# An eight-expert attention model on one core: scores in halves of 64 keys, expert columns prepared earlier, the last division in pieces

## The chip, the cores and the metric

The kernel runs on one core of a Trainium2 chip. The metric is device time in microseconds of one execution. A core has five engines with a queue each: TensorE (PE in the profile, with its weight loads apart as PEld), VectorE (DVE), ScalarE (ACT), GpSimd (POOL) and SyncE (SP). Products go from PE into PSUM, eight banks of 512 float32 per partition; everything else lies in SBUF or in the chip's main memory.

## What is computed

The input is one image of 256 channels and 64 by 64 pixels. Layer 0 is a linear attention over boxes of pixels, layer 1 a softmax attention over all 4096 tokens and a mixture of eight experts with two experts per token.

```python
# layer 0
x = x + L0_conv(_gn(x))               # q, k sigmoid, v normalized; for boxes of 64, 32, 16 pixels:
                                      #   attn = q . box(k v) / (q . box(k) + 1e-6); then Wout
# layer 1
t = _to_tokens(x)                     # 4096 tokens of 256
t = t + L1_attn(_ln_t(t))
t = t + L1_ffn(_ln_t(t))
...
# L1_attn, 8 heads of 32
qkv = x @ w_qkv + b_qkv
dots = einsum('bhid,bhjd->bhij', q, k) * d ** -0.5
out = softmax(dots) @ v ;  return out @ w_out + b_out
# L1_ffn, 8 experts, 2 per token
logits = xt @ Wr + br
xe = xn * ln_g[e] + ln_b[e]
h = gelu(xe @ W1[e] + b1[e]);  y = h @ W2[e] + b2[e]
out = sum over the two best experts of weight * y
```

Everything is float32.

## The kernel before

**Order of the work.** The code states the work in program order; a planner then orders each engine's queue by its own estimates, so that neighbouring steps of independent work may stand in the queue in another order than in the code. `tc.issue_after` ties an instruction behind another one of its engine. Waits between engines are semaphores. What stands inside a branch isn't mixed with what stands outside.

**Layer 0** (`prepare`, `attend`) runs twice, for four heads each time (g = 0, 1). `prepare` makes q, k, v and sums by boxes. `attend` walks over three box sizes and computes scores of key tiles against strips of query columns, four heads at a time: head h has its 32 channels on partitions 32h to 32h + 31, so that the four heads' products use four row groups of PE. Strips are packed into steps of at most 512 columns. One part (L612, box sizes with r above 1) computes scores 64 keys at a time, since keys of the upper and the lower half of a tile have different queries. The other part (L681) computes 128 keys at a time. `masked` (L557, L561) multiplies the scores by masks on DVE, ACT and POOL, and `use` (L643, L697) multiplies by v. In the L681 part a step consists of one or two pieces: those of 384 or 512 columns stand alone, those of 192 and 256 share a step.

**Layer 1, q, k, v.** For eight chunks c of 512 tokens: normalize, transpose (`to_channels`, L779 and L780), project q and k (L885, copied out by L889), project v together with the router's columns (L896, L903, L904). This part has a pool of PSUM tiles `mm` of four banks and a pool `a_in` called `win`. At its end a bound on all scores is computed and read into a register, `tame`.

**Layer 1, attention.** A branch on `tame` holds two versions; the first one runs with this input. It has 16 blocks, one for each chunk of 512 queries (qc) and each group of four heads (g). A block walks over 32 key tiles i. Per tile:

```python
sc = [two_banks() for _ in range(2)]          # 2 of 3 double banks
for hd in range(4):
    nc.tensor.matmul(sc[hd // 2][:, hd % 2, :], qk[hs, 1, g, tok(i)], qk[hs, 0, g, chunk(qc)], ...)   # L994
for pair, s in zip(pairs, sc):
    nc.scalar.activation(pe[:, pair, :], s, AF.Exp, ...)                                              # L1004
for pair in pairs:
    add = nc.vector.tensor_add(total[:, pair, :], ..., pe[:, pair, :])                                # L1011, i = 1 to 30
```

The values' product `use` (L962, into `ps_acc`) of a tile is emitted one tile later, by `tick`. `pe` has four buffers, `total` one. For the softmax's denominators, the last tile's `pe` (in `take`) and then `total` (in `whole`) are multiplied by ones into `ps_den` (both L962). `take` also copies the accumulator to `attnT` (L1029). For 15 blocks the denominators then travel through main memory to be inverted compactly (`pack`, `turn`, `spread`, L1050 to L1063). For the last block `divide` inverts them at once: one reciprocal of 128 by 512 (L1040) and one product (L1035), and then `project` runs for the last four token tiles (L943, L946, and the statistics of the second normalization, L764 and L765). Of the other 28 token tiles four are projected in each block with g = 1 from qc = 1 on.

**Behind the branch.** The phase of the experts begins with constants (L129), the router's bias `br` (L151) and a block named `routing`. That one first loads three matrices of the experts (b1, ln_g, ln_b) as rows, transposes them on PE (L1207), copies them on DVE (L1208) into `cols`, and stores `cols` to main memory as `crows` (L1212), from where each slot of the expert phase loads its expert's columns (L1184). Then come the second normalization (`norm2.begin`: L769 and the square root L770; `end`: L773), the normalized rows (L1229) and their store `zrows`, the choice of two experts per token, the places of all tokens in the slots (L1352 to L1401), and the expert phase proper (L1413 to L1466) with the final sum and transposes.

**What ACT's tables need.** Exp, square root, sigmoid and gelu each make ACT load a table when the function before was another one (ACT_TABLE_LOAD in the profile).

Of the kernel before, what the change touches and what calls it, by code (L numbers as in the profile page):

```python
# [22 lines left out]
F32 = mybir.dt.float32  # L23
# [7 lines left out]
P = 128  # L31
# [83 lines left out]
def tile_conv_attn_hybrid(ctx: ExitStack, tc: tile.TileContext, a: dict, out: bass.AP):  # L115
# [73 lines left out]
    with ExitStack() as phase:  # L189
# [394 lines left out]
        def attend(g, work, ps, qk, v, ssum, rec, woT):  # L584
# [6 lines left out]
            for w in (2, 1, 0):  # L591
# [71 lines left out]
                for ix in range(NCH):  # L663
# [12 lines left out]
                    for step in steps:  # L676
                        scs = [score() for _ in range(4)]
                        at, places = 0, []
                        for n, i, c0, c1, *mk in step:
                            for h in range(4):  # L680
                                nc.tensor.matmul(  # L681
                                    scs[h][:, at : at + n],
                                    kT[hs[h], tok(i)],
                                    qT[hs[h], CH * ix + CELL * c0 : CH * ix + CELL * c1],
                                    start=True,
                                    stop=True,
                                    skip_group_check=True,
                                )
                            places.append((at, n, i, c0, c1, *mk))
                            at += n  # L690
                        sms = masked(work, scs, at, joined((p[0], p[1], *p[-2:]) for p in places))
                        step_done()

                        def use(places=places, sms=sms, acc=acc, begun=begun, ix=ix, last=step is steps[-1], raw=raw, r=r):
                            for at, n, i, c0, c1, *_ in places:
                                for h in range(4):
                                    nc.tensor.matmul(  # L697
                                        acc[hs[h], CELL * c0 : CELL * c1],
                                        v[:, i, hs[h]],
                                        sms[h][:, at : at + n],  # L700
                                        start=not begun[0],
                                        stop=last and at == places[-1][0],
                                        skip_group_check=True,
                                    )
                                begun[0] = True
                            if last and r > 1:
                                nc.vector.tensor_add(raw[:, ix, :], acc, raw[:, ix, :])
                            elif last:
                                nc.scalar.copy(raw[:, ix, :], acc)

                        behind(lambda: None, use)
# [68 lines left out]
        nc.scalar.copy(dst, tp[:, :C].rearrange("p (k n) -> p k n", k=KC))  # L780

    norm2 = Norm(keep, "ln2")


    with ExitStack() as phase:
# [15 lines left out]
        with (  # L801
# [61 lines left out]
            for c in range(NCH):  # L863
# [29 lines left out]
                for i in range(NB * c, NB * (c + 1)):  # L893
# [8 lines left out]
                        )  # L902
                    nc.vector.tensor_add(v[:, i, :], pv[:, :C], bv)  # L903
                    nc.scalar.copy(t[:, i, C:], pv[:, C : C + NE])  # L904


            on_experts = lambda z: z.unsqueeze(2).to_broadcast([P, NT, NE])
# [41 lines left out]
        with tc.If(tame > 0) as branch:  # L949
            with (  # L950
# [33 lines left out]
                for qc in range(NCH):  # L984
                    for g in range(KC):
# [4 lines left out]
                        for i in range(NT):  # L990
                            sc = [two_banks() for _ in range(2)]
                            for hd in range(4):
                                hs = slice(D * hd, D * (hd + 1))
                                nc.tensor.matmul(  # L994
                                    sc[hd // 2][:, hd % 2, :],
                                    qk[hs, 1, g, tok(i)],
                                    qk[hs, 0, g, chunk(qc)],
                                    start=True,
                                    stop=True,
                                )  # L1000
                            pe = work.tile([P, 4, CH], F32, name="pe", bufs=4)
                            pairs = [slice(0, 2), slice(2, 4)]
                            for pair, s in zip(pairs, sc):
# [20 lines left out]
                            if i == NT - 1:  # L1024
# [9 lines left out]
                                def times(rec, to=to):  # L1034
                                    nc.vector.tensor_mul(to, to, rec)  # L1035

                                def divide(den=den, whole=whole, times=times):
                                    whole()
                                    rec = work.tile([P, CH], F32, tag="rec", name="rec")
                                    nc.vector.reciprocal(rec, den[0])  # L1040
                                    times(rec)

# [100 lines left out]
    with ExitStack() as phase:  # L1145
# [3 lines left out]
        small = pool("m_small", 1)  # L1149


        cst.update(constants_of("m", wts))
        zrows = dram.tile([N, C], F32, name="zrows")
        yrows = dram.tile([2 * N + NU * P, C], F32, name="yrows")


        crows = dram.tile([NE, P, NH + 2 * KC], F32, name="crows")
        br = row_on_all("L1_ffn_br", NE, wts)

        def each(name):  # L1160
# [34 lines left out]
        with ExitStack() as routing:  # L1195
# [1 line left out]
            r_ps = routing.enter_context(psum("r_ps", 2))  # L1197
            bank, _ = banks(r_ps)
            r_work = pool("r_work", 2)

            cols = r_work.tile([P, NE, NH + 2 * KC], F32, name="cols", bufs=1)
            at = 0
            for name, n in (("L1_ffn_b1", NH), ("L1_ffn_ln_g", KC), ("L1_ffn_ln_b", KC)):
                rw = r_work.tile([NE * n, P], F32, tag="rw", name=f"{name}_rows")
                nc.scalar.dma_start(rw, a[name].rearrange("e (k p) -> (e k) p", p=P))
                tp = bank()
                nc.tensor.transpose(tp[:, : NE * n], rw, ident[: NE * n, : NE * n])  # L1207
                nc.vector.tensor_copy(  # L1208
                    cols[:, :, at : at + n], tp[:, : NE * n].rearrange("p (e k) -> p e k", e=NE)
                )  # L1210
                at += n
            nc.scalar.dma_start(crows.rearrange("e p n -> p e n"), cols)  # L1212

# [331 lines left out]
```

## Time and profile before

| | |
|---|---|
| median of 3 runs | 2913.63 us (2911.81 to 2914.61) |
| profiled execution: its time | 2911.62 us |
| its span, first to last instruction | 2909.8 us |
| layer 0 | 0 to 1029 us |
| q, k, v of layer 1 | 1029 to 1153 us |
| attention, with the last projections | 1153 to 2325 us |
| routing | 2325 to 2371 us |
| experts and output | 2371 to 2910 us |
| PE busy, share of the span | 2769.2 us, 95% |
| DVE busy | 2082.3 us, 72% |
| ACT busy | 1529.6 us, 53% |
| POOL busy | 712.4 us, 24% |

How to read the profile: times are microseconds of one profiled execution. A group's row gives the line, the engine, the operation, output and inputs by the program's names, the shapes and the number of instructions; behind the first bar stand the busy time in all and the mean nanoseconds of one; behind the second the time that the engine sat idle just before these instructions, and what ended it. A timeline's row gives start, length, engine, line and operation, the number of merged instructions, and in brackets the idle time ahead of it. A float32 matmul of the code appears as two MATMUL records[...], each with a weight load of its own (LDWEIGHTS on PEld). Matmuls overlap, so that their lengths don't add up. Instants of single instructions are given from the start of the span.

### The profile page before, as it was taken

To read this page: it belongs to the slowest core of one execution; us is meant where nothing else is said; L and a number is where in the kernel's file an instruction comes from. 1 tells how busy PE (TensorE), PEld (TensorE's weight loads), DVE (VectorE), ACT (ScalarE), POOL (GpSimd) and SP (SyncE) were. 2 spreads that over 40 slices of the span, in tenths; PEclk is the share of its full clock that TensorE was granted. 3 is DMA by queue.
4 is the path that set the end of the run, shared out by engine and by line. 5 is a ranking of instruction groups with operands and counts; after the bars stand their busy time and mean duration, and the time that the engine had idled before them with its cause. 6 is when DMAs were issued, how large, how long until landed. Compare 5 with 4: busy or idle time off the path is not lost. (4 is left out here: it accounts for less than half of the span.)

```text
span 2909.8 us, 62928 instructions
## 1 busy us (share of the span) xinstructions
PE 2769.2 (95%) x26286; PEld 1329.9 (46%) x26286; DVE 2082.3 (72%) x3009; ACT 1529.6 (53%) x2134; POOL 712.4 (24%) x808
## 2 busy tenths in 40 slices
PE   6899999989999988999999999999999969999996
PEld 5466442735644254222222222222222248888884
DVE  6776777577676886999999999999999941111113
ACT  3242323124233312888888888888888642222222
POOL 1085858109485711000000000000000012222220
PEclk9999999999999999999999999999999969999997
DMA  5000000000000000000000000000000056565665
GB/s 143 6 2 3 2 3 2 7 0 3 4 2 3 1 19 1 1 5 6 5 5 5 5 5 5 5 5 5 5 5 5 10 176 215 190 203 196 205 213 189
DMA packets 97546, 136.31 MB, mean 47 GB/s; under 512 B 18115, under 2 KB 79145, under 8 KB 97253
## 3 DMA queue, kind: packets, MB, share of 16 engines
q1 hardware_dynamic: 82360, 105.34, 11.2%
q0 software_dynamic: 6528, 17.83, 2.2%
q10 hardware_dynamic: 8364, 9.02, 0.9%
q8 instruction: 209, 3.42, 0.5%
q14 instruction: 85, 0.69, 0.1%
HBM read 114.57 MB, written 17.60 MB: 45 GB/s over the span
## 5 line engine op out<-in xcount | busy, mean ns | idle before, releaser
L1004 ACT ACTIVATE pe<-ps_two 128x1024 f32<-128x1024 f32 x1024 | 993.1, 1022 | 152.2 <-PE ps_two L994 146.9
L1011 DVE TENSOR_TENSOR total<-total,pe 128x1024 f32<-128x1024 f32 x928 | 1058.2, 1219 | 2.2 <-ACT pe L1004 2.2
L994 PE MATMUL ps_two<-qk 32*128 32x512 f32 x4096 | 630.6, 640 | 3.5 <-POOLq L949 1.8
L962 PE MATMUL ps_acc<-pe,v 128*32 128x512 f32 x4096 | 547.2, 605 | 0.1
L557 ACT COPY sm<-ps_sc 128x384 f32<-128x384 f32 (+4 forms) x486 | 232.5, 513 | 460.6 <-PE ps_sc L681 271.2
L561 POOL TENSOR_TENSOR sm<-sm,mask 128x192 f32<-128x192 f32 (+3 forms) x460 | 380.2, 860 | 232.7 <-ACT sm L557 232.5
L994 PEld LDWEIGHTS ps_two<-qk 32*128 32x128 f32 x4096 | 205.2, 183 | 419.5 <-PE ps_two L994 221.3
L561 DVE TENSOR_TENSOR sm<-ps_sc,mask 128x384 f32<-128x384 f32 (+3 forms) x708 | 324.1, 518 | 92.8 <-PE ps_sc L681 91.4
L1456 ACT ACTIVATE hid<-ps_hp,cols 128x256 f32<-128x256 f32 (+1 forms) x288 | 133.1, 462 | 360.4 <-PE ps_hp L1453 359.3
L1271 POOL MEMSET on<- 128x256 f32 x1 | 0.3, 311 | 1177.3 <-PE ps_den L962 1177.3
L962 PEld LDWEIGHTS ps_acc<-pe,v 128*32 128x32 f32 x4096 | 80.8, 108 | 390.3 <-issue 377.2
L681 PE MATMUL ps_sc<-qk 32*128 32x192 f32 (+3 forms) x2688 | 245.3, 446 | 5.7 <-DVE sm L561 2.9
L1453 PE MATMUL ps_hp<-xe,w 128*128 128x256 f32 (+1 forms) x1152 | 246.6, 370 | 0.0
L1462 PE MATMUL ps_yp<-w,hid 128*128 128x256 f32 x1088 | 240.8, 379 | 0.0
L1453 PEld LDWEIGHTS ps_hp<-xe,w 128*128 128x128 f32 x1152 | 201.1, 190 | 39.7 <-ACT hid L1456 5.6
L697 PE MATMUL ps_acc<-sm,v 128*32 128x192 f32 (+3 forms) x2688 | 216.6, 423 | 0.8 <-POOL sm L561 0.8
L1462 PEld LDWEIGHTS ps_yp<-w,hid 128*128 128x128 f32 x1088 | 204.2, 190 | 26.4
L1432 DVE TENSOR_SCALAR xe<-ps_tp,cols 128x256 f32<-128x256 f32 (+1 forms) x72 | 34.8, 525 | 239.3 <-PE ps_tp L1428 217.5
L561 POOL TENSOR_TENSOR sm<-sm,ycut 128x384 f32<-128x384 f32 (+4 forms) x150 | 150.8, 1024 | 140.9 <-ACT sm L557 140.6
L681 PEld LDWEIGHTS ps_sc<-qk 32*128 32x128 f32 x2688 | 126.3, 186 | 124.5 <-DVE sm L561 70.1
L561 DVE TENSOR_TENSOR sm<-ps_sc,ycut 128x512 f32<-128x512 f32 (+4 forms) x250 | 127.7, 562 | 65.2 <-PE ps_sc L612 63.2
L1464 DVE TENSOR_TENSOR y<-ps_yp,b 128x256 f32<-128x256 f32 x68 | 28.9, 425 | 195.1 <-PE ps_yp L1462 195.1
(239 smaller groups left out, 2244.3 us busy)
## 6 DMA issues: line engine op xcount, KB each, us to landing
w<-in_L_ffn_W SPq DMA_DIRECT2D x72, 1024.0 KB
b<-in_L_ffn_b SPq DMA_DIRECT2D x36, 128.0 KB
rows<-in_x SPq DMA_DIRECT2D x16, 256.0 KB
zrows<-act SPq DMA_DIRECT2D x4, 1024.0 KB
y<-yrows SPq DMA_DIRECT2D x8, 512.0 KB
y<-yrows ACTq DMA_DIRECT2D x8, 512.0 KB
rec<-recs SPq DMA_DIRECT2D x60, 64.0 KB
x<-in_x ACTq DMA_DIRECT2D x4, 512.0 KB
```

What stands on the lines that cost most here:

```text
L557: nc.scalar.copy(sm[:, :used], sc[:, :used])
L561: engine.tensor_mul(to, of, mk.unsqueeze(1).to_broadcast(list(to.shape)))
L681: nc.tensor.matmul(scs[h][:, at : at + n], kT[hs[h], tok(i)], qT[hs[h], CH * ix + CELL * c0 : CH * ix + CELL * c1], start=True, stop=True, ...
L697: nc.tensor.matmul(acc[hs[h], CELL * c0 : CELL * c1], v[:, i, hs[h]], sms[h][:, at : at + n], start=not begun[0], stop=last and at == plac ...
L962: nc.tensor.matmul(to[D * hd : D * (hd + 1), :], lhsT(hd), rhs[:, hd, :], start=start, stop=stop, skip_group_check=True,)
L994: nc.tensor.matmul(sc[hd // 2][:, hd % 2, :], qk[hs, 1, g, tok(i)], qk[hs, 0, g, chunk(qc)], start=True, stop=True,)
L1004: nc.scalar.activation(pe[:, pair, :], s, AF.Exp, scale=C**-0.5)
L1011: add = nc.vector.tensor_add(to, first[:, pair, :] if i == 1 else to, pe[:, pair, :])
L1432: nc.vector.tensor_scalar(xe[:, k, :n], tp[:, k, :n], cols[:, gain], cols[:, shift], op0=ALU.mult, op1=ALU.add,)
L1453: nc.tensor.matmul(hp[:, :n], w1[:, k, tok(m)], x_now[:, k, :n], start=k == 0, stop=k == KC - 1)
L1456: nc.scalar.activation(hid[:, m, :n], hp[:, :n], AF.Gelu, bias=cols[:, m : m + 1])
L1462: nc.tensor.matmul(yp, hid[:, m, tok(j)], w2[:, m, :], start=m == 0, stop=m == NH - 1)
```

## The change

Five edits:

1. In layer 0 a step of the L681 part with a single piece computes its scores in two halves of 64 keys; steps with two pieces stay at 128.
2. In the attention each head's scores (L994) are computed in two halves of 64 keys. The tiles in PSUM stay as they were.
3. The last block's division runs in four pieces of 128 queries, each a reciprocal and a product.
4. The experts' columns leave the routing. A function `expert_columns` loads, transposes, copies (now on ACT) and stores them after chunk c = 2 of the q, k, v part, with loads and the store in SP's queue and PSUM tiles from the four banks `mm`.
5. The first instruction behind the branch on ACT is a square root of one element, `root`.

```diff
                         for n, i, c0, c1, *mk in step:
+
+                            rows = CELL if len(step) == 1 else P
                             for h in range(4):
-                                nc.tensor.matmul(
-                                    scs[h][:, at : at + n],
-                                    kT[hs[h], tok(i)],
...
+                                for u in range(0, P, rows):
+                                    nc.tensor.matmul(
+                                        scs[h][u : u + rows, at : at + n],
+                                        kT[hs[h], P * i + u : P * i + u + rows],
...
+    def expert_columns(pool, ps):
+        cols = pool.tile([P, NE, NH + 2 * KC], F32, name="cols")
+        at = 0
+        for name, n in (("L1_ffn_b1", NH), ("L1_ffn_ln_g", KC), ("L1_ffn_ln_b", KC)):
+            rw = pool.tile([NE * n, P], F32, name=f"{name}_rows")
+            nc.sync.dma_start(rw, a[name].rearrange("e (k p) -> (e k) p", p=P))
+            tp = ps.tile([P, CH], F32, tag="mm", name="ps_mm")
+            nc.tensor.transpose(tp[:, : NE * n], rw, ident[: NE * n, : NE * n])
+            nc.scalar.copy(cols[:, :, at : at + n], tp[:, : NE * n].rearrange("p (e k) -> p e k", e=NE))
+            at += n
+        nc.sync.dma_start(crows.rearrange("e p n -> p e n"), cols)
...
+                if c == 2:
+                    expert_columns(win, ps)
...
-                                nc.tensor.matmul(
-                                    sc[hd // 2][:, hd % 2, :],
-                                    qk[hs, 1, g, tok(i)],
...
+                                for u in range(2):
+                                    nc.tensor.matmul(
+                                        sc[hd // 2][CELL * u : CELL * (u + 1), hd % 2, :],
+                                        qk[hs, 1, g, P * i + CELL * u : P * i + CELL * (u + 1)],
...
                                     rec = work.tile([P, CH], F32, tag="rec", name="rec")
-                                    nc.vector.reciprocal(rec, den[0])
-                                    times(rec)
+                                    for n in range(CH // P):
+                                        nc.vector.reciprocal(rec[:, tok(n)], den[0][:, tok(n)])
+                                        nc.vector.tensor_mul(to[:, tok(n)], to[:, tok(n)], rec[:, tok(n)])
...
+        root = small.tile([1, 1], F32, name="root")
+        nc.scalar.sqrt(root, ident[:1, :1])
...
-            for name, n in (("L1_ffn_b1", NH), ("L1_ffn_ln_g", KC), ("L1_ffn_ln_b", KC)):
-                rw = r_work.tile([NE * n, P], F32, tag="rw", name=f"{name}_rows")
-                nc.scalar.dma_start(rw, a[name].rearrange("e (k p) -> (e k) p", p=P))
-                tp = bank()
-                nc.tensor.transpose(tp[:, : NE * n], rw, ident[: NE * n, : NE * n])
-                nc.vector.tensor_copy(
...
-            nc.scalar.dma_start(crows.rearrange("e p n -> p e n"), cols)
```

## The prediction

> **What bounds the kernel now.** I read the page first, then the table of stretches, the groups of the attention stretch, the timelines of VectorE and TensorE at one block's end, two score steps of layer 0, and the stretch behind the attention. The head of the page:
>
> ```profile
> span 2909.8 us, 62928 instructions
> ...
> PE 2769.2 (95%) x26286; PEld 1329.9 (46%) x26286; DVE 2082.3 (72%) x3009; ACT 1529.6 (53%) x2134; POOL 712.4 (24%) x808
> ```
>
> TensorE (PE) looks like the bound of everything. In the table of stretches, however, from 1600 to 1900 us PE is busy for all 300.00 us and VectorE (DVE) for 291.90. A PE busy without a gap can be waiting inside, so the attention (1153 to 2319 us, 40% of the span) needs a closer look. Its groups:
>
> ```profile
> L1011 DVE TENSOR_TENSOR total<-total,pe 128x1024 f32<-128x1024 f32 x928 | 1058.2, 1219 | 2.2 <-ACT pe L1004 2.2
> L1004 ACT ACTIVATE pe<-ps_two 128x1024 f32<-128x1024 f32 x1024 | 993.1, 1022 | 152.2 <-PE ps_two L994 146.9
> L994 PE MATMUL ps_two<-qk 32*128 32x512 f32 x4096 | 630.6, 640 | 3.5 <-POOLq L949 1.8 <-ACT pe L1004 1.6
> L962 PE MATMUL ps_acc<-pe,v 128*32 128x512 f32 x4096 | 547.2, 605 | 0.1
> ```
>
> The 928 running sums of L1011 waited 2.2 us in all: inside a block (one qc, one g, 32 key tiles) DVE never waits. It waits only at a block's end, where `total` must be read by PE before the next block overwrites it:
>
> ```profile
> 1247.40 47.77 DVE L1011 TENSOR_TENSOR total<-total,pe 128x1024 f32<-128x1024 f32 x42
> 1296.98 2.36 DVE L1011 TENSOR_TENSOR total<-pe 128x1024 f32<-128x1024 f32 x2 [1.81 <-ACT pe L1004]
> ```
> ```profile
> 1292.81 1.04 PE L962 MATMUL ps_den<-pe,ones 128*32 128x512 f32 x8
> 1293.78 1.14 PE L994 MATMUL ps_two<-qk 32*128 32x512 f32 x8
> 1294.85 1.06 PE L962 MATMUL ps_acc<-pe,v 128*32 128x512 f32 x8
> 1295.73 1.04 PE L962 MATMUL ps_den<-total,ones 128*32 128x512 f32 x8
> 1296.70 1.14 PE L994 MATMUL ps_two<-qk 32*128 32x512 f32 x8
> ```
>
> The last sum ends at 1295.17. PE, which works through its queue without a gap, reaches the products that read `total` at 1295.73, 0.56 us late, and DVE starts again 1.25 us after that. So the attention is DVE's sums end to end, plus a gap at each of 15 block ends, part of which is PE being late. The waits list has these gaps as 29.8 us (13 times) behind `pe` and 7.4 (4 times) behind `ps_den`; without the 6.1 us before the first sum and the 2.2 above, 29 us for 15 ends: 2.73 at the first, 1.78 to 2.06 at the others.
>
> Layer 0 (0 to 1029 us) is PE's. Its scores exist in both forms, 64 keys at a time (L612) and 128 (L681), here both with 384 query columns:
>
> ```profile
> 385.25 0.90 PE L612 MATMUL ps_sc<-qk 32*64 32x384 f32 x16
> 386.08 0.98 PE L643 MATMUL ps_acc<-sm,v 64*32 64x448 f32 x16
> ```
> ```profile
> 475.99 0.93 PE L681 MATMUL ps_sc<-qk 32*128 32x384 f32 x8
> 476.84 1.07 PE L697 MATMUL ps_acc<-sm,v 128*32 128x512 f32 x8
> ```
>
> From a step's start to the next line's is 0.83 us with 64 keys, 0.85 with 128, though there are twice the instructions. Behind the attention DVE carries the chain:
>
> ```profile
> 2315.24 3.36 DVE L1040 RECIPROCAL rec<-ps_den 128x512 f32<-128x512 f32 x1 [1.15 <-PE ps_den L962]
> 2318.71 0.69 DVE L1035 TENSOR_TENSOR act<-act,rec 128x512 f32<-128x512 f32 x1
> ...
> 2324.68 0.30 DVE L765 BATCH_NORM_AGGREGATE ln_mv<-st 128x2 f32<-128x6 f32 x2
> ...
> 2327.72 0.17 DVE L1283 TENSOR_SCALAR steps<-cstm 128x16 f32<-128x16 f32 x1 [2.74 <-issue]
> ...
> 2328.13 0.31 DVE L1208 COPY cols<-ps_mm 128x64 f32<-128x64 f32 x2 [0.24 <-DMA L_ffn_ln_b_rows<-in_L_ffn_ln_b]
> 2328.35 0.17 DVE L769 TENSOR_SCALAR ln_rstd<-ln_mv 128x32 f32<-128x32 f32 x1
> ```
>
> **What the Trainium skill says.** "TensorE: Matmul & The Clock Gate", LDWEIGHTS (loading the stationary operand): a load takes columns/1.2 ns, whatever the rows. That is 107 ns for 128 columns, 53 for 64, 27 for 32. The trace agrees: an f32 product runs as two passes, and in L994 the second starts 533 ns after the first (427 of stream, 106 of load), in L962 454 after (427 and 27), in L612 with 448 columns 427 after (373 and 54). The same page, The mechanism: a load overlaps running matmuls only in other row groups. The trace agrees for the first pass to the second, but from the second pass on a step's further loads are hidden (162 ns from pass to pass at 192 columns, with either form). "TensorEngine Tiling (Array Packing)", Instruction Overhead: about 60 cycles per matmul. The trace is far below that: matmuls on different tiles start 6.7 ns apart, in L612 eight in 47 ns. "ScalarE: Activation LUTs", What ACT_TABLE_LOAD costs: 1283 ns and a drain; the load before the root at 2326.05 us took 1.28.
>
> **Scores in the attention, removed and added.** Each of 512 iterations exchanges 8 matmuls with 128-column loads for 16 with 64-column loads. Between the passes 107 − 53 = 54 ns go. As eight matmuls start over 47 ns instead of four over 20, the last one ends 27 ns later, and the next kind starts 91 ns behind the end of the last stream in both forms. PE saves 54 − 27 = 27 ns per iteration; single starts at 384 columns give 857 − 831 = 26. Heads 2 and 3 often start later than 0 and 1 because they wait for exp; a pair then has its second matmul's stagger only, so up to 40 ns are saved. Over 32 iterations that is 0.8 to 1.3 us per block. DVE's sums don't get shorter (960 × 1.14 us), so it can be cashed only at the block ends: with PE there in time, the gap is 1.25 us plus some 0.05 for the signal, 1.30. The fourteen later gaps, 26.3 us together, lose 26.3 − 14 × 1.30 = 8.1, needing 0.5 to 0.8 us of PE per block, which it has. The first end (2.73, PE slowed at the start) is limited by PE and gets about 1.0. **−9.1 us**; bounds −10 and, should PE's saving be eaten elsewhere, 0.
>
> **Scores in layer 0.** Only steps of one piece are split: 80 of 384 columns and 32 of 512 (640 and 256 matmul records by 8). 112 × 26 ns = 2.9. In 48 of them heads 2 and 3 wait some 0.07 to 0.2 us for their bank, so a part comes back as waiting. **−2.5**, bounds −3.5 and 0.
>
> **Last division in pieces.** A reciprocal costs 0.553 us at 64 columns (L345) and 3.353 at 512 (L530), by interpolation 0.95 at 128; a product of 128 columns 0.29 (L1287), the hand-over 0.11 (2318.71 − 2318.60), less some 0.05 of overlap: 1.3 per piece, 5.2 for four against 4.16. DVE is through at 2320.4 instead of 2319.4. But PE may start the first of the last four token tiles at 2316.6. Before, these tiles took DVE from 2319.40 to 2324.98, of which 1.06 + 0.45 + 0.75 us went in waiting for PE; 3.3 us are work. 2320.4 + 3.3 = 2323.7: **−1.2**, bounds 0 (if the pieces' small hand-overs cost double) and −2.3.
>
> **Columns moved out of the routing.** Three copies, three transposes, three row loads and the store of `crows` leave. L769, the first step of the chain to the routing, stood behind the copies at 2328.35; it can start at about 2327.85, behind the 2.74 us that DVE stands still after the branch and which stay. One later copy (0.17 us, 0.12 from start to start) also lay in the chain. **−0.6**, bounds 0 and −1.
>
> **Columns added at c = 2.** PE is busy 18.97 of 20 us from 1060 on; three transposes at 0.17 us from start to start (L1207) are **+0.5**, bounds 0 and +1.5 (each also holds one of four banks till ACT has copied it). The three copies (0.2 us each) lie on an ACT that is busy 2.8 of 20 us. The four DMAs go to SP's queue, which is empty between the weights at 1029.86 and the attention's own from 1225 on; nobody behind them waits. Without that cover the rows' 2 to 3 us to land would stand before the first transpose.
>
> **Root behind the branch.** The table load before, at 2326.05, ended 1.2 us ahead of L769's result, so it was hidden; earlier it is hidden too: 0. ACT has only the load of `br` queued behind it, needed at 2329.95. If the 1.28 us ever lay open, that is its price.
>
> **Sum.** −9.1 − 2.5 − 1.2 − 0.6 + 0.5 = −12.9 us. The profiled execution has a span of 2909.8 and took 2911.62: 2896.9 and 2898.7. Its time lies 2.0 under the median of the runs shown, 2913.63; against that median the forecast is **2900.7**.
>
> **The rivals.** First, the attention gives nothing: PE's 27 ns disappear in its loop with exp, and the gaps stay at 1.8. Speaking for it: ACT waited 146.9 us for scores, PE's score loads waited behind other scores 221.3 us, so the loop has its own rhythm (2.16 us per iteration against 2.07 of PE's work). Against: that rhythm contains the shortened pass. It gives 2913.6 − 3.8 = 2909.8. Second, only half comes: 2905. Third, on the other side: the planner that orders each engine's queue sees eight score products for four, counts PE as slower than it is, and puts the products of `total` one iteration later. (That it reorders shows at 1030 us, where two L764 stand before two L765 though the code alternates.) Each of 15 ends would then cost one more turn of scores and values, 2.1 us: +31 − 3.8, thus 2941; even a fifth of the ends misplaced would eat most of the rest. Against it: at every end the products stand directly behind the values, as written. Fourth, the split doesn't do what it says, because eight streams of 512 columns don't run side by side; then 0.43 us more per pass, hundreds of us. L612 with 448 columns excludes it nearly: less than 1 in 100.
>
> **Numbers.** Forecast 0.72; half 0.10; nothing in the attention 0.10; planner 0.05; every bound on the good side (−16.8, about 2897), 0.03. A measurement of this kernel can't tell 0.2% (5.8 us) from no change, so the line lies at 2907.8. Faster are the forecast, the half and the best case, 0.85; same 0.10; slower 0.05. The range reaches from 2895.0 (all bounds good, less the 1.8 us by which the lowest run lies under the median) to 2908.5, beyond the half and short of the first rival.
>
> **What would show it.** Second pass of L994's successor 480 ns after the first; gaps before `total<-pe` of 1.3 instead of 1.8 to 2.0; DVE's sums unchanged in number and at 1.14 us; a single-piece step of 384 columns 0.83 us long; 8.5 us from the last division's first reciprocal to the last L765 instead of 9.7; L769 directly behind `steps`. Wrong would make it: gaps still at 1.8, a DVE that waits inside a block, or L994's two passes still 533 apart.

## The result and the profile after

| kernel | median us | range, runs | ratio to the kernel before |
|---|---|---|---|
| before | 2912.81 | 2910.74 to 2914.61, 6 | |
| changed | 2902.53 | 2899.56 to 2903.15, 6 | 0.9962 [0.9950, 0.9975] |

The change saves 10.3 us; 12.9 were forecast. The heads of the pages, after:

```profile
span 2900.4 us, 73149 instructions
...
PE 2758.0 (95%) x31278; PEld 1283.2 (44%) x31278; DVE 2081.5 (72%) x3012; ACT 1529.1 (53%) x2138; POOL 712.6 (25%) x808
```

There are 10,221 instructions more. The groups of the attention stretch (busy, mean ns of one, then idle time ahead and who ended it):

```profile
L1035 DVE TENSOR_TENSOR total<-total,pe 128x1024 f32<-128x1024 f32 x928 | 1058.1, 1215 | 1.2 <-ACT pe L1028 1.1
L1028 ACT ACTIVATE pe<-ps_two 128x1024 f32<-128x1024 f32 x1023 | 991.5, 1021 | 144.0 <-PE ps_two L1017 128.2 <-DVE total L1035 0.2
L1017 PE MATMUL ps_two<-qk 32*64 32x512 f32 x8168 | 619.1, 613 | 1.8 <-ACT pe L1028 1.8
L983 PE MATMUL ps_acc<-pe,v 128*32 128x512 f32 x4096 | 547.1, 605 | 0.1
```

The sums (L1035, before L1011) and the values (L983, before L962) are as they were; the scores have twice the records. In the trace's single starts the second pass of the scores begins 480 ns behind the first where nothing holds it (533 before). The end of the second block (the one shown of before), on DVE and on PE (start, length, then idle time ahead):

```profile
1250.23 47.78 DVE L1035 TENSOR_TENSOR total<-total,pe 128x1024 f32<-128x1024 f32 x42
1299.22 2.36 DVE L1035 TENSOR_TENSOR total<-pe 128x1024 f32<-128x1024 f32 x2 [1.21 <-PE ps_den L983]
```
```profile
1295.77 1.11 PE L1017 MATMUL ps_two<-qk 32*64 32x512 f32 x16
1296.81 1.07 PE L983 MATMUL ps_acc<-pe,v 128*32 128x512 f32 x8
1297.69 1.42 PE L983 MATMUL ps_den<-total,ones 128*32 128x512 f32 x8
1299.04 1.11 PE L1017 MATMUL ps_two<-qk 32*64 32x512 f32 x16
```

The last sum ends at 1298.01. PE reaches the products of `total` at 1297.69, ahead of it, and has to wait for it: the eight last 1.42 us instead of 1.04. The gap is 1.21 us instead of 1.81. At the later ends PE is still just too late: the products start 0.10 us (g = 0) and 0.20 us (g = 1) behind the last sum, typically 0.56 and 0.74 before. The gaps are 1.26 and 1.43 us there, 2.69 at the first end, and the 15 add up to 21.4 us, 29.0 before. One single-piece step in layer 0, followed by its neighbour's values:

```profile
449.97 0.90 PE L684 MATMUL ps_sc<-qk 32*64 32x384 f32 x16
450.80 0.77 PE L643 MATMUL ps_acc<-sm,v 64*32 64x320 f32 x16
```

From start to start 0.83 us, as forecast. Behind the attention:

```profile
2310.50 1.77 DVE L1065 RECIPROCAL rec<-ps_den 128x128 f32<-128x128 f32 x2 [1.18 <-PE ps_den L983]
2312.18 0.42 DVE L1066 TENSOR_TENSOR act<-act,rec 128x128 f32<-128x128 f32 x2
...
2317.35 0.30 DVE L768 BATCH_NORM_AGGREGATE ln_mv<-st 128x2 f32<-128x6 f32 x2
2320.32 0.17 DVE L1296 TENSOR_SCALAR steps<-cstm 128x16 f32<-128x16 f32 x1 [2.67 <-issue]
2320.40 0.17 DVE L772 TENSOR_SCALAR ln_rstd<-ln_mv 128x32 f32<-128x32 f32 x1
```

From the first reciprocal to the last L768 (before L765) 7.15 us pass, 9.74 before; L772 (before L769) stands directly behind `steps`, as the forecast wanted it.

**Stage by stage.** The runs of this study leave different parts of the code as before, so each stage can be read from several profiles. A stage runs from one marker to the next: layer 0 from its first score to the last sum of its output product; q, k, v to the attention's first score; the attention to the last division's first reciprocal; the division to the last L765 or L768; the last one to the first row that ACT normalizes with `less`.

```
stage            forecast  profiles with the old code  profiles with the new code    difference
layer 0            -2.5    888.5 (5: 884.6 to 892.1)   888.4 (7: 886.0 to 889.9)       -0.1
q, k, v            +0.5    117.5 (5: 116.7 to 118.5)   118.7 (8: 117.9 to 119.6)       +1.2
attention          -9.1    1167.5 (2: 1167.0, 1168.0)  1159.9 (9: 1157.8 to 1161.4)    -7.6
division           -1.2    8.94 (5: 8.18 to 9.74)      7.15 (9: all 7.15)              -1.8
to the routing     -0.6    7.05 (5: 6.99 to 7.20)      6.61 (9: 6.44 to 7.21)          -0.4
```

The sum is -8.7; the two profiles' spans differ by 9.4 and the medians by 10.3. One code's profiles spread by 1 to 4 us in the long stages, in the old layer 0 by 7.5. The rest can't be told from that spread, and the -0.1 of layer 0 alone says little: it has to be read step by step.

### The profile page after: what moved, and what is told of

The parts are those of the page before. It is cut to its first block, busy times and chain, and to the rows that moved or that the text cites. A ratio compares the mean times of both kernels' runs of the same rounds, so it can differ in the third digit from the quotient of the medians.

```text
span 2900.4 us, 73149 instructions
## 1 busy us (share of the span) xinstructions
PE 2758.0 (95%) x31278; PEld 1283.2 (44%) x31278; DVE 2081.5 (72%) x3012; ACT 1529.1 (53%) x2138; POOL 712.6 (25%) x808
## 3 DMA queue, kind: packets, MB, share of 16 engines
q8 instruction: 248, 4.06, 0.6%
## 4 chain that ended last, share of the span: by engine, by line
PE 57%; DVE 1%; DMA 1%; issue 0%; SPq 0%; ACT 0%; POOL 0%; ACTq 0%; POOLq 0%; DVEq 0%
PE ps_two L1017 20%; PE ps_acc L983 18%; PE ps_hp L1466 8%; PE ps_yp L1475 8%; PE ps_den L964 1%; PE ps_den L983 1%; DMA y<-yrows 1%; PE ps_tp L1441 1%; DVE t L1518 0%; DMA b<-in_L_ffn_b 0%; DMA yrows<-y,target 0%; DMA xs<-zrows,source 0%; DVE rec L1065 0%; POOL xs L1426 0%; PE ps_mm L1524 0%
## 5 line engine op out<-in xcount | busy, mean ns | idle before, releaser
L1035 DVE TENSOR_TENSOR total<-total,pe 128x1024 f32<-128x1024 f32 x928 | 1058.1, 1215 | 1.2 <-ACT pe L1028 1.1
L1017 PE MATMUL ps_two<-qk 32*64 32x512 f32 x8192 | 621.0, 613 | 3.6 <-POOLq L970 1.8
L983 PE MATMUL ps_acc<-pe,v 128*32 128x512 f32 x4096 | 547.1, 605 | 0.1
L1017 PEld LDWEIGHTS ps_two<-qk 32*64 32x64 f32 x8192 | 166.0, 130 | 422.2 <-PE ps_two L1017 377.3
L983 PEld LDWEIGHTS ps_acc<-pe,v 128*32 128x32 f32 x4096 | 80.7, 108 | 417.3 <-issue 403.3
L684 PE MATMUL ps_sc<-qk 32*64 32x384 f32 (+3 forms) x3584 | 241.1, 462 | 4.6 <-DVE sm L561 2.9
L684 PEld LDWEIGHTS ps_sc<-qk 32*64 32x64 f32 (+1 forms) x3584 | 116.8, 159 | 122.9 <-DVE sm L561 70.1
```

Of the source, the lines that this page charges most:

```text
L684: nc.tensor.matmul(scs[h][u : u + rows, at : at + n], kT[hs[h], P * i + u : P * i + u + rows], qT[hs[h], CH * ix + CELL * c0 : CH * ix + C ...
L983: nc.tensor.matmul(to[D * hd : D * (hd + 1), :], lhsT(hd), rhs[:, hd, :], start=start, stop=stop, skip_group_check=True,)
L1017: nc.tensor.matmul(sc[hd // 2][CELL * u : CELL * (u + 1), hd % 2, :], qk[hs, 1, g, P * i + CELL * u : P * i + CELL * (u + 1)], qk[hs, 0, g ...
L1035: add = nc.vector.tensor_add(to, first[:, pair, :] if i == 1 else to, pe[:, pair, :])
```

## The experiments

### One part alone, and one part undone

**Only the attention's scores**, in the kernel before:

```
+    for u in range(2):
         nc.tensor.matmul(
-            sc[hd // 2][:, hd % 2, :], qk[hs, 1, g, tok(i)], qk[hs, 0, g, chunk(qc)],
+            sc[hd // 2][CELL * u : CELL * (u + 1), hd % 2, :],
+            qk[hs, 1, g, P * i + CELL * u : P * i + CELL * (u + 1)], qk[hs, 0, g, chunk(qc)],
...
```

> The kernel before with only the attention's scores (L994) in halves of 64 keys. Theory A (PE was late at the block ends, the halves bring it there in time): gaps of VectorE at the fifteen block ends fall from 29.0 us in all to about 21.4 as in the changed kernel, the stretch from the first score to the last division is 8 to 9 us shorter, layer 0 and the rest stay, ratio about 0.997. Rival B (the gain came from the whole program's other order or placing and not from the halves): under 3 us, ratio 0.999 or above.

Measured: 2904.69 us, 0.9973 [0.9962, 0.9984] of the kernel before, 2912.51 beside it. That is 7.8 us for this part alone, and its 15 gaps are 21.2 us in all, those of the changed kernel.

**Without the halves in layer 0**, in the changed kernel:

```
-    rows = CELL if len(step) == 1 else P
+    rows = P
```

> The changed kernel with layer 0's single-piece scores at 128 keys again. Theory A (112 steps save 26 ns each and nothing takes it back): layer 0 gets 2.5 to 3 us longer, so that its stretch is about 891.5 us against 888.9. Theory C (TensorE runs out of instructions in the following stretches of small products, because the halves need more instructions, and that eats the gain): layer 0 stays or gets up to 1 us shorter, 887 to 889 us, with fewer and shorter gaps of TensorE in the L612 and L643 stretches.

Measured: 2903.01 us, 0.9961 [0.9947, 0.9975]. The times can't tell it from the changed kernel. Its layer 0 took 892.1 us in the profile against 889.5, which looks like the forecast gain; but three more profiles of the old layer 0 (884.6, 886.4, 891.0) take that reading back. What the halves do has to be read from steps that come in the same order in all traces; this is done below.

**With the columns back in the routing** (the call at c = 2 taken out, the old block put back) and **with the last division whole** (one reciprocal and one product for the four pieces):

> The changed kernel with the experts' columns prepared in the routing as before. Theory A: the q, k, v stretch loses 0.5 us (three transposes) and the routing gains 0.6, no change in all. Theory D (the early row load delays the weights and biases of the q, k, v part by 0.9 us, and one more window of half clock follows from it by chance): the q, k, v stretch, from layer 0's last sum to the first score, falls from 120.3 to about 117.9 us, with the biases' product 5.9 us behind layer 0's last product instead of 6.8; the routing takes 0.6 more; in all 1.8 us faster than the changed kernel.

> The changed kernel with the last division whole. Theory A as predicted: from the reciprocal's start to the last L765 group 9.6 us again instead of 7.0, the whole kernel 2.6 us slower (1.2 by the prediction's sum), ratio to the kernel before about 0.997. Rival E (the shorter way comes from something else at the branch's end, not from the pieces): unchanged at 7.0.

Measured: 2902.26 us, 0.9961 [0.9948, 0.9975], and 2904.53 us, 0.9971 [0.9958, 0.9983]. With the columns in the routing, the stage to the routing is 6.99 us again and q, k, v 117.6; the time itself can't tell theory A (no change) from theory D (1.8 us less). With the division whole, the division takes 8.18 us, not the 9.74 of the kernel before, though DVE's instructions are the same. The difference stands in PE's last output products, one line of each kernel, the kernel before first:

```profile
2319.45 4.18 PE L943 MATMUL ps_two<-wo,act 128*128 128x264 f32 x10 [2.72 <-DVE act L1035]
```
```profile
2312.77 2.49 PE L964 MATMUL ps_two<-wo,act 128*128 128x264 f32 x10 [2.75 <-DVE act L1065]
```

The same ten matmuls took 4.18 and 2.49 us. The view by stretches (length, busy times, then PEclk, DMA share, GB/s), again the kernel before first, gives the reason:

```profile
2319.40:2323.70 4.30, 4.18 (x10) 2.96 (x10) 2.04 (x8) 0.00 (x0) 1.04 (x1) 0.60 0.06 15
```
```profile
2312.70:2315.30 2.60, 2.49 (x10) 1.81 (x10) 1.78 (x7) 0.00 (x0) 1.04 (x1) 1.00 0.03 6
```

The granted clock was 0.60 in one and 1.00 in the other. "TensorE: Matmul & The Clock Gate" of the Trainium skill, Part 1, says that the clock is halved or full by a free-running window of 3413 ns, which sees how busy PE was; the traces agree: their half-clock stretches last 3.41 us or multiples of it (but for the last, which the end of the run cuts) and lie elsewhere from profile to profile. PE's pause of 2.7 us for a whole division falls into such a window in some profiles (9.74, 9.17, 9.42 us) and not in others (8.18 twice). With pieces PE pauses 0.51 and 0.86 us; in all nine profiles the clock stays full through the stage, which takes 7.15. So the pieces by themselves are worth 1.0 us, and 1.8 in the mean, most likely because they also close the pause in which the clock can fall.

### Who sets a block: one sum less for VectorE

The forecast said that the attention is DVE's sums end to end. If so, 2.28 us less of sums must show. In the kernel before and in the changed kernel (the denominators then lack one key tile in 32):

```
-    elif i < NT - 1:
+    elif i < NT - 1 and i != 2:
```

> The kernel before with the two running sums of key tile 2 left out of each block: the denominators lack the exponentials of one key tile in 32, so the output differs from the reference; TensorE's and ScalarE's work stays. It frees VectorE of 2 x 1.14 = 2.28 us per block. The prediction's view (a block is VectorE's sums end to end plus the gap at its end): a block of g = 0 goes from 70.72 us to 68.4, the gap at the end grows only where TensorE is late. Rival (TensorE's loop with the exponentials sets the block, VectorE's sums fill it by chance: the products of total ran 0.56 us late): the block stays at 70.2 to 70.7 and the gap at its end, or waits inside, take up the 2.28 us.

> The changed kernel with the same two sums per block left out (denominators lack one key tile in 32). Its block against that of the kernel before with one sum less is TensorE's own saving per block without VectorE as a limit. The prediction: 0.8 to 1.3 us per block (27 to 40 ns per iteration). Rival (the exponentials start later behind eight score products with four that signal than behind four with two, which takes a part back): 0.54 us per block or less (17 ns per iteration), the size by which the products of total came earlier.

Measured, first sums of two successive blocks (the period of a block of g = 0): before, before with one sum less, changed, changed with one sum less.

```profile
1442.57 2.36 DVE L1011 TENSOR_TENSOR total<-pe 128x1024 f32<-128x1024 f32 x2 [1.97 <-ACT pe L1004]
1513.29 2.36 DVE L1011 TENSOR_TENSOR total<-pe 128x1024 f32<-128x1024 f32 x2 [1.80 <-ACT pe L1004]
```
```profile
1440.20 2.36 DVE L1011 TENSOR_TENSOR total<-pe 128x1024 f32<-128x1024 f32 x2 [2.39 <-ACT pe L1004]
1510.93 2.36 DVE L1011 TENSOR_TENSOR total<-pe 128x1024 f32<-128x1024 f32 x2 [2.25 <-ACT pe L1004]
```
```profile
1443.78 2.36 DVE L1035 TENSOR_TENSOR total<-pe 128x1024 f32<-128x1024 f32 x2 [1.41 <-ACT pe L1028]
1513.95 2.36 DVE L1035 TENSOR_TENSOR total<-pe 128x1024 f32<-128x1024 f32 x2 [1.26 <-ACT pe L1028]
```
```profile
1442.04 2.36 DVE L1035 TENSOR_TENSOR total<-pe 128x1024 f32<-128x1024 f32 x2 [1.81 <-ACT pe L1028]
1512.22 2.36 DVE L1035 TENSOR_TENSOR total<-pe 128x1024 f32<-128x1024 f32 x2 [1.73 <-ACT pe L1028]
```

The periods are 70.72, 70.73, 70.17 and 70.18 us. Taking 2.28 us from DVE gave nothing here, in either kernel; DVE only waits more (30.2 us inside the blocks of the kernel before in place of 2.2):

```profile
L1011 DVE TENSOR_TENSOR total<-total,pe 128x1024 f32<-128x1024 f32 x896 | 1021.8, 1214 | 30.2 <-ACT pe L1004 30.2
```

**So the forecast's bound was wrong: PE's loop with exp sets the block, before and after.** DVE's own length lies close below, at 70.13 us (68.92 of sums and the gap of 1.21 at the one end where PE was early), which is why it seemed to be the bound. In that one block DVE does set the length in the changed kernel: 70.13 us, and 69.82 with one sum less. Everywhere else the change shortens PE's loop by 0.54 us per block, and 16 blocks give 8.6. What is left between the two is 0.05 us per block: a further gain needs both engines.

How much of the shorter pass arrives, from the starts of scores (S) and values (V) in the middle of seven blocks of g = 0, nearly 200 iterations per profile:

```
kernel                      S to V, mean ns   same, nothing in the way   V to S   iteration
before                           1162.9              1070                 995.9    2158.8
before, one sum less             1163.0              1070                 995.8    2158.8
changed                          1146.7              1044                 995.8    2142.5
changed, again                   1146.8              1044                 995.7    2142.4
```

Unhindered, a step of scores is 26 ns shorter, as forecast (27). In the loop 16 arrive, since the wait inside the step grew from 93 to 103 ns. The single starts show it ahead of heads 2 and 3, and the likely cause is the PSUM bank that exp frees: three double banks serve four head pairs in flight.

### Is it that wait? Shorter exponentials

Exp over 448 of 512 columns, the rest of `pe` filled by GpSimd, and two tiles' sums left out, so that neither ScalarE nor VectorE holds the loop:

```
+    nc.gpsimd.memset(pe[:, :, CH - CELL :], 1.0)
...
-    nc.scalar.activation(pe[:, pair, :], s, AF.Exp, scale=C**-0.5)
+    nc.scalar.activation(pe[:, pair, : CH - CELL], s[:, :, : CH - CELL], AF.Exp, scale=C**-0.5)
...
-    elif i < NT - 1:
+    elif i < NT - 1 and i not in (2, 4):
```

> The kernel before with the exponentials of the attention taken over 448 of 512 columns (the other 64 columns of pe are filled with ones by GpSimd) and the sums of key tiles 2 and 4 left out, so that neither ScalarE nor VectorE can hold the loop; the output differs from the reference. TensorE's work stays. Theory (the loop is TensorE's steps plus a wait of its third and fourth score product for the bank that exp frees, 0.09 us per iteration of 2.16): 2.07 us per iteration, a block of g = 0 67.8 to 68.3 instead of 70.72. Rival (exp doesn't hold TensorE): 70.7.

> The changed kernel with the same: exponentials over 448 of 512 columns, sums of key tiles 2 and 4 left out. Theory (17 of 27 ns per iteration arrive in the loop because the rest is waited away for exp): without that wait 27 ns per iteration arrive, the block is 0.8 to 0.9 us shorter than that of the kernel before with the same edits. Rival (the shorter pass is worth 17 ns by itself, the wait has no part): 0.5 to 0.6 us shorter, as unedited.

Measured: periods of 69.84 and 69.43 us, steps from S to V of 1140.1 and 1123.4 ns. Both theories of the second run missed: the two kernels differ by 0.41 us per block, less than the 0.5 to 0.6 of the lower one. Exp became 0.10 us shorter (0.92 instead of 1.02), but it also started later, in the mean 0.10 us behind the start of the values in the kernel before and 0.13 in the changed one, instead of 0.03 and 0.05, perhaps because it now waits for the fill too. The wait fell by 23 ns only, and still 17 ns of the 26 arrive. The pair shows that exp's length reaches PE's loop (0.9 us per block in the kernel before, 0.75 in the changed one). It does not show where the other 10 ns go; that stays open.

### Halves for two heads only

Heads 0 and 1 with 128 keys, heads 2 and 3 with 64:

```
-    for u in range(2):
+    rows = CELL if hd > 1 else P
+    for u in range(0, P, rows):
...
```

> The changed kernel with the attention's scores 64 keys at a time only for heads 2 and 3; heads 0 and 1 have 128 keys in one product again. The prediction's working: the passes of heads 0 and 1 are 533 ns apart again, so the step is as long as before unless heads 2 and 3 end it; the block between 70.2 and 70.7 us, time +0 to +8 us against the changed kernel. Rival (later start of exp eats 10 to 20 ns per iteration): exp of heads 0 and 1 starts as early as before behind two products, heads 2 and 3 keep the shorter pass; block 69.8 to 70.1, time -1 to -3.

Measured: 3459.41 us, 1.1896 [1.1880, 1.1912]. Both theories missed by hundreds of microseconds. Three steps of the loop:

```profile
1499.73 1.61 PE L1018 MATMUL ps_two<-qk 32*128 32x512 f32 x10
1501.28 1.06 PE L983 MATMUL ps_acc<-pe,v 128*32 128x512 f32 x8
1502.27 2.15 PE L1018 MATMUL ps_two<-qk 32*128 32x512 f32 x12
1504.35 1.07 PE L983 MATMUL ps_acc<-pe,v 128*32 128x512 f32 x8
```

A step of scores takes 2.08 us from start to start instead of 1.15. The two pairs of heads no longer run side by side: the first pass of heads 2 and 3 starts 0.52 us behind the second of heads 0 and 1. "TensorEngine Tiling (Array Packing)", Key Properties, has the sentence: "Changing tiling mode (not just tile) drains the TensorE". Here 32x128 and 32x64 in one group are two modes, and the trace agrees at 0.9 us per step. That makes 30 us per block. The first block took 187.2 us instead of 72.3: there the granted clock stayed at 0.50 from 1148.7 to 1336.4 us, though PE shows no gap; some 115 of the 560 us come from this. The change was harmless because it switched all four heads together.

### Where the gain in layer 0 went

The steps of layer 0 come in the same order in all fourteen profiles, so step can be set against step. The 80 single-piece steps with 384 columns fell from 858 to 832 ns (median), the 32 with 512 from 1089 to 1051, 3.2 us together, and the values behind them grew by 0.3 us in all: -2.9 us, the 112 x 26 ns of the forecast. But three other steps, whose code is untouched, grew. They are the values (L643) behind the local-sum products L631 in the second stretch with 64 keys:

```
         whole scores (5 profiles)  |  halves (7 profiles)
first    0.59 in each               |  1.33  1.27  1.35  0.99  0.95  1.33  1.20
second   0.59 in each               |  2.22  1.99  1.95  1.68  2.24  1.71  1.69
third    0.59 in each               |  1.99  1.69  1.97  1.71  2.00  1.99  2.02
```

(us from start to start.) The mean growth is 3.3 us, all of the gain. Other steps moved too, single ones by up to 1.6 us between the means of the two groups, but up and down, by -0.5 us in all. The second of the three places, in the kernel before and in the changed kernel:

```profile
419.96 1.99 PE L631 MATMUL ps_acc<-qk,ssum 32*32 32x64 f32 x128
421.88 0.66 PE L643 MATMUL ps_acc<-sm,v 64*32 64x256 f32 x16
422.47 1.01 PE L612 MATMUL ps_sc<-qk 32*64 32x448 f32 x16
```
```profile
421.12 0.94 PE L612 MATMUL ps_sc<-qk 32*64 32x384 f32 x16
421.99 1.99 PE L631 MATMUL ps_acc<-qk,ssum 32*32 32x64 f32 x128
423.90 0.66 PE L643 MATMUL ps_acc<-sm,v 64*32 64x256 f32 x15
425.80 0.40 PE L643 MATMUL ps_acc<-sm,v 64*32 64x256 f32 x1 [1.24 <-issue]
```

In the changed kernel PE stops after 15 of 16 matmuls that wait for nothing ("issue"). The DMA queue that carries instructions shows why. Its lines in the pages before and after:

```profile
q8 instruction: 209, 3.42, 0.5%
```
```profile
q8 instruction: 248, 4.06, 0.6%
```

39 packets more carry the 9,984 loads and matmuls that PE has more: 256 each. (With the attention's halves alone it is 32 packets and 8,192, 256 again.) One such packet landed at 424.36, and PE went on 1.44 us later; the next stop of this kind (1.00 us) ended 1.36 us after the packet that landed at 440.06. L631 alone takes 256 instructions, 128 loads and 128 matmuls, in 1.99 us: one packet. If PE runs dry because a packet's end falls there, then the stops have fixed places in the count of PE's instructions. They have. With all of PE's records (loads, matmuls and waits) numbered from 0 in order of their starts, the three restarts in the changed kernel are 12,225, 12,993 and 13,761: each is 193 above a multiple of 256. In all of layer 0, of the pauses above 0.25 us that end 1.15 to 1.70 us behind a packet's landing:

```
kernel                        pauses   at remainder 193   at any other remainder, most
before                            75                 22                              4
changed                           90                 25                              3
```

So the kernel before has such stops too, in other places. The halves did not create them but moved them, and three came to lie in a stretch that had none. Where they lie depends on how many instructions stand ahead. A kernel that leaves only the first eight single-piece steps of layer 0 whole has 128 fewer:

```
+    singles = []
...
+    singles.append(len(step) == 1)
-    rows = CELL if len(step) == 1 else P
+    rows = CELL if len(step) == 1 and sum(singles) > 8 else P
```

> The changed kernel, but the first 8 single-piece steps of layer 0 in the first group of heads have whole scores again: 8 x 16 = 128 instructions less ahead of everything later, half of a 256-instruction fetch packet; costs 8 x 0.028 = 0.2 us. Theory (TensorE runs dry where a packet's end meets the dense 64-key steps, which depends on how many instructions lie ahead): the three gaps in front of the last values of the second 64-key stretch (0.59 us each before, 1.33, 2.22 and 1.99 in the changed kernel, 3.8 us in all) shrink or move; time -3 to 0. Rival (the higher rate of instructions in the steps just before causes them): the three gaps stay within 0.3 us, time +0.2.

Measured: 2895.61 us beside 2907.88 of the kernel before, 0.9958 [0.9944, 0.9971]. The same place:

```profile
418.10 0.94 PE L613 MATMUL ps_sc<-qk 32*64 32x384 f32 x16
418.96 1.99 PE L632 MATMUL ps_acc<-qk,ssum 32*32 32x64 f32 x128
420.88 0.66 PE L644 MATMUL ps_acc<-sm,v 64*32 64x256 f32 x16
```

The three stops are gone, with the same 64-key steps and the same rate of instructions; 18 pauses stand at remainder 193. Layer 0 took 883.5 us, 4.4 under the changed code on the same chip (887.9, in the run with one sum less), but only 1.1 under the old code there (884.6, in the kernel before with one sum less), so one profile of the stage doesn't measure the gain; the steps do. **So the halves' gain in layer 0 is real, 2.9 us by its own steps, and was lost to an instruction supply whose packet ends moved into a dense place.**

### Both repairs together

> The changed kernel unchanged, timed beside the next one: 0.9962 of the kernel before, 11 us faster. In its trace the last values ahead of the three gaps of the second 64-key stretch of layer 0 take more than 0.59 us again, 1.5 to 3.8 us above it in all.

> The changed kernel with both repairs: the first 8 single-piece steps of layer 0 whole (no gap in front of the last values of the second 64-key stretch, layer 0 3 to 4 us shorter, as in the run before), and the experts' rows loaded at the kernel's start into one tile of 96 rows, so one transpose at c = 2 in place of three and no row load beside the bias rows. Theory (the rows' load delays the bias rows by 0.9 us and the three transposes cost 0.5): the bias product stands 5.2 us behind the last sum of layer 0 instead of 6.1, and the q, k, v stage is 1.0 to 1.4 us shorter; time 4 to 5 us under the changed kernel. Rival (the bias rows come late for another reason, the half clock): the bias product stays at 5.6 to 6.1, time 3 to 4 us under it.

The second kernel keeps the eight whole steps and loads the experts' rows at the start:

```
+    e_rows = keep.tile([NE * (NH + 2 * KC), P], F32, name="expert_rows")
...
+            nc.sync.dma_start(e_rows[at : at + NE * n], a[name].rearrange("e (k p) -> (e k) p", p=P))
...
+        nc.tensor.transpose(tp[:, : e_rows.shape[0]], e_rows, ident[: e_rows.shape[0], : e_rows.shape[0]])
...
-            nc.sync.dma_start(rw, a[name].rearrange("e (k p) -> (e k) p", p=P))
...
-            nc.tensor.transpose(tp[:, : NE * n], rw, ident[: NE * n, : NE * n])
```

Measured: the changed kernel 2900.55 us (2899.51 to 2902.96), 0.9965 [0.9951, 0.9979]; the repaired one 2896.49 us (2894.39 to 2899.43), 0.9949 [0.9935, 0.9962]. Their ranges don't meet, if only by 0.1 us; the repaired kernel is 4.1 us faster than the changed one. It has none of the three stops, layer 0 took 885.1 us (887.9 in the changed kernel beside it), and q, k, v 117.5 where the changed code takes 117.9 to 119.6. How the 4.1 us divide between the two repairs was not timed side by side. Its bias product stands 5.45 us behind layer 0's last sum, between the 5.2 of the theory and the 5.6 to 6.1 of the rival. That place alone proves little: it lies at 5.2 to 6.1 us with the rows loaded beside it (mean 5.8) and at 5.2 to 5.9 with the rows in the routing (mean 5.4).

## Why the prediction was right, and which steps were not

The time fell into the range, on the forecast side, 1.8 us above the forecast (2902.5 against 2900.7). The shorter pass, the size of its saving and the place where it shows were right; that the sum came so near is in part luck, since a bound that was wrong gave the right size for the attention and a loss in layer 0 was partly made up by the clock in the division. By its steps:

- **The attention, -9.1:** 7.8 alone and 7.6 by stages, 8.6 by 16 block periods; the right size. The step "the attention is DVE's sums end to end" failed: with 2.28 us less of sums a block stays at 70.73 us. PE's loop sets it, and the gap at the block's end was the mark of PE's lateness, not a loss of its own. The forecast gap of 1.30 us was met (1.21 to 1.43 from the second end on) because the 0.54 us that PE gained per block is nearly what it had been late (0.56, 0.74); nothing in the forecast's reasons made these two alike. "0.8 to 1.3 us per block" was too much: 16 of 26 ns per iteration arrive. The first rival, that the loop with exp swallows the gain, was right for 10 ns of them.
- **Layer 0, -2.5:** about 0. The 112 steps gave their 2.9 us. The deduction for heads that wait was not the one needed: 3.3 us went into stops for instructions, which the forecast did not price at all, though the kernel before shows 22 of them.
- **The division, -1.2:** -1.8 in the mean, -1.0 at a full clock. The pieces were priced at 5.2 us on DVE and took 4.1, no more than the whole (0.89 per reciprocal, and 0.42 for two products), and the clock's share was not seen.
- **Columns out of the routing, -0.6:** 0.4 in the mean, 0.6 between the two profiles shown.
- **Columns at c = 2, +0.5:** +1.2 by stages. The three transposes are the 0.5 (0.57 us from their start to the next product's); in the mean the bias product comes 0.4 later. The rest is most likely the clock, by chance: the half-clock stretch at the stage's start lasts 13.7 us in most profiles and 17.1 in others, three of eight with the columns and one of five without. Among those with 13.7 us the stage takes 118.3 us with the columns (five profiles) and 117.3 without (four); the longer stretch adds about 1.0. "Nobody behind them waits" looked at SP's queue alone. The planner put the first row load far ahead of c = 2, in the same microsecond as the bias rows' two loads on ACT's queue (first fence SP, second ACT, changed kernel):

```profile
1031.79 0.58 SPq L796 DMA_DIRECT2D L_ffn_b_rows<-in_L_ffn_b  x1
```
```profile
1031.33 0.60 ACTq L831 DMA_DIRECT2D bias_rows<-in_L_attn_b_qkv  x1
1031.97 0.26 ACTq L832 DMA_DIRECT2D bias_rows<-in_L_attn_b_out  x1
```

That they delay each other is likely and was not shown: the places of the bias product overlap.
- **The root, 0:** its table load now stands at 2309.52, in ACT's pause, and L773, its first user, still starts right behind L772. It was not tried by itself.
- **The planner's rival** (2941) did not come: at every block end the products of `total` stand behind the values. The rival of halves that don't run side by side did not come for four equal heads; the kernel with halves for two heads shows that it was one edit away.

## What to carry to other kernels

An engine whose operations follow each other without a gap is not thereby the bound: take some of its work away and see whether the period moves. Count a split in instructions too, not only in nanoseconds per step: where PE takes more than a hundred instructions per microsecond, the gain of one place can be paid in another that was not touched, and 128 instructions less ahead brought it back here. Number an engine's instructions and look at the remainder of its pauses: that tells a stop of the supply from a wait. Tiles of different sizes in one group of matmuls took turns here.

## What was not expected of the hardware

- Where PE's instructions came at some 128 per microsecond, it stopped at one place of a 256-instruction cycle (remainder 193), for 1.2 us in the case shown, and went on 1.2 to 1.6 us after the landing of a packet. A packet has 16 KB (4.06 MB in 248) and carries 256 instructions.
- 32x128 and 32x64 products in one step: 2.08 us; all four heads alike, of either size: 1.15 to 1.16.
- Ten matmuls took 2.49 or 4.18 us by whether a pause of 2.7 us ahead of them met a half-clock window.
